# Two GNN layers on one core: rows normalized in one ScalarE pass, and seven of layer 1's blocks in seven products

## The chip, the cores and the metric

The kernel runs on one core of a Trainium2 chip. The engines of a core work side by side, each through its own list of instructions in order: TensorE (PE) multiplies matrices, VectorE (DVE) and ScalarE (ACT) work elementwise, GpSimd (POOL) does small elementwise work and issues gathers, SyncE (SP) issues transfers. They wait for each other by semaphores. The metric is the device time of one execution in microseconds (us), and lower is better. "Time" below is that; a "span" is the time from the first to the last instruction of a profiled execution.

## The reference

Two layers of a graph transformer over N = 2708 nodes with 512 features, 8 heads of 64, and a feed-forward part of width 2048, all in float32. The adjacency matrix has about nine entries in a row. Cut to one layer, which is applied twice with its own weights:

```python
mask = adj + eye(n)
q, k, v = h @ Wq.T + bq, h @ Wk.T + bk, h @ Wv.T + bv        # 8 heads of 64
scores = einsum('nhd,mhd->hnm', q, k) / sqrt(64)
attn = softmax(where(mask == 0, -1e9, scores))
ctx = einsum('hnm,mhd->nhd', attn, v).reshape(n, 512)
h1 = layer_norm(h + ctx @ Wo.T + bo, ln1_g, ln1_b)
ff = relu(h1 @ W1.T + b1) @ W2.T + b2
h2 = layer_norm(h1 + ff, ln2_g, ln2_b)
```

layer_norm subtracts a row's mean, divides by the square root of its variance plus 1e-5, and then multiplies by a gain and adds a shift.

## The kernel before

**Attention by lists.** The kernel makes for each node a list of its neighbours, sorts the nodes by the length of their lists into 22 tiles of 128 rows (the last has 20), and gathers the keys and values of the neighbours from DRAM, a row of 1024 numbers for each node and list place. The longest list of each tile is a constant (CAPS, 3 to 22 places). Attention over a tile runs in chunks of two places: POOL gathers the rows into a buffer kv (L1114), DVE multiplies them by q (L1151) and sums by heads to the scores sc (L1157), ACT takes exponentials p (L1170) and weights the second place's values (L1177), DVE weights the first place's (L1183) and adds both into acc (L1190). ACT's and DVE's last part of a chunk is written behind the scores of the next chunk. At a tile's end DVE adds the two halves and makes the divisor (L1198 to L1213), and ACT writes the context cx (L1221). Gathers are asked about four chunks ahead. The context of a tile lies in one of CXB = 3 places until it is used; attention stops when all are full.

**Blocks.** The 22 tiles are worked off as 11 blocks of two, blocks 0 to 10. A block's feed-forward part is a loop over 16 steps f of 128 hidden numbers each. In a step PE makes pf (the product with W1, four matmuls 128x256, L1578 or L1720), and ACT makes ft = relu(pf + b1) (L1589 or L1731). In a plain block PE adds, three steps behind, ft's product with W2, two matmuls of 128x512 (L1551).

**Seven products.** In blocks 2 to 9 of layer 0 (FORMED = 1 is the last plain one ahead of them), feed_forward_by_seven takes the steps in pairs j = 0 to 6. The pair's product with W2 is a 2x2 product of blocks, which takes eight half-width matmuls of 128x256 when done plainly. It is done in seven (L1710), by Winograd's scheme. For that DVE makes four sums of parts of ft for each pair (L1687 to L1690), written ahead of the chunks of the same step; four sums of W2's quarters are needed for each pair. Three of them (forms) lie in DRAM (form_d) and are loaded by SP for each pair and block (L1672), the fourth (t1) takes W2's quarter b12 in its place. They are made in block 1 (form, L1649 to L1659). At a block's end DVE puts the partial sums together (L1763 to L1768). Steps 14 and 15 stay plain (L1740, L1744).

**Beside the steps.** While block k goes through its steps, the other work is hung into the steps by hand. At f = 10 PE turns the context of the next block's first tile (tp<-cx, L1336) and ACT moves it to cT (L1341); at f = 11 comes its output projection o (L621), then DVE's total h of o and the residual (L1294), the turn of the second tile, and ACT's sum of squares (L1311); at f = 12 the same for the second tile; at f = 13 and 14 the normalization; at f = 15 PE turns the rows (tp<-h) and ACT moves them to hT. The block before has its second normalization (ended) at the steps of TAILS; in layer 0 its rows are then turned (f = 7) and multiplied for layer 1's keys and values (f = 8 and 9, four projections), and written out. In layer 1 they go straight to the output.

**Normalization.** Norm.total has DVE add and sum the row, squares has ACT sum the squares, centred has POOL make the power -1/2 (L1318, L1320) and DVE subtract the mean and multiply by the gain (L1321), scaled has ACT multiply by the power (L1327). Where rows are turned, ACT adds the shift from a column as it moves them. In row form the shift is added by a DMA of POOL's queue that accumulates (L1330). The other form, norm, does all on DVE (L1270 to L1283), for the first and the last block of a layer.

**Order.** The order on each engine is that in which the program writes the instructions. How much attention is written into a step is set by tables: PACE for plain blocks, PACE7 for blocks by seven products, PACES for block 0; 1.0 is one chunk of two places. A context that isn't there when it is needed is finished on the spot (until).

**Border.** In layer 0's last block (10) SP loads layer 1's W1 and W2 as the old ones become free. After it PE projects layer 1's queries until the first contexts are there.

Of the kernel before, what the change touches and what calls it, by code (L numbers as in the profile page):

```python
# [13 lines left out]
ALU = mybir.AluOpType  # L14
# [40 lines left out]
PACE7 = (0.0,) * 4 + (0.6,) + (1.3,) * 4 + (0.6,) * 2 + (0.0,) * 2 + (0.5, 0.8, 2.4)  # L55
TAILS = ((0, 1, 5, 6), (3, 4, 5, 6), (0, 1, 2, 3, 5, 8))
FORMED = 1
# [427 lines left out]
def by_edges(ctx: ExitStack, tc: tile.TileContext, x, xT, adj, layers, out, redo):  # L485
# [71 lines left out]
    form_d = dram.tile([NFC // 2 - 1, 3, P, 2 * P], F32, name="form_d")  # L557
# [582 lines left out]
    class Tile:  # L1140
# [75 lines left out]
        def divided(self):  # L1216
            r = self.r
            cx = at.tile([P, DM], F32, tag="cx", name="cx", bufs=CXB)
# [47 lines left out]
    def norm(z, r, gain, shift=None, st=None):  # L1266
# [9 lines left out]
        nc.gpsimd.tensor_tensor(rd[:r], va[:r], mhalf[:r], ALU.pow)  # L1276
        nc.vector.scalar_tensor_tensor(
            z[:r], z[:r], mv[:r, 0:1], gain[:r], ALU.subtract, ALU.mult
        )
        if shift is None:  # L1280
            nc.vector.tensor_scalar(z[:r], z[:r], rd[:r], None, ALU.mult)
            return
        nc.vector.scalar_tensor_tensor(z[:r], z[:r], rd[:r], shift[:r], ALU.mult, ALU.add)  # L1283

    class Norm:


        def __init__(self, z, r, gain, junk):
            self.z, self.r, self.gain, self.junk = z, r, gain, junk
# [25 lines left out]
        def centred(self):  # L1315
            r, z, nm = self.r, self.z, self.nm
# [4 lines left out]
            nc.vector.scalar_tensor_tensor(  # L1321
                z[:r], z[:r], nm[:r], self.gain[:r], ALU.add, ALU.mult
            )

        def scaled(self):
            r, z = self.r, self.z
            nc.scalar.activation(z[:r], z[:r], AF.Copy, scale=self.rd[:r])  # L1327
# [4 lines left out]
    def flip(z, r, to, shift=None):  # L1332
# [7 lines left out]
        for c in range(NC):  # L1340
            nc.scalar.activation(  # L1341
                to[:, c, :], tp[:, c, :r], AF.Identity, bias=shift[:, c : c + 1]
            )

    class Layer:
# [5 lines left out]
        def load_first(self):  # L1351
# [7 lines left out]
            self.unsettled = raw_columns(w, ("bv", "ln1_b"), place)  # L1359
            self.bv, self.e1 = [col[0] for col in self.unsettled]  # L1360
# [44 lines left out]
        def load_next(self):  # L1405
# [4 lines left out]
            self.unsettled += raw_columns(self.w, ("ln2_b",), place)  # L1410
            self.e2c = self.unsettled[-1][0]
# [64 lines left out]
        def attended(self, block, got, xbs=None, soon=False):  # L1476
# [16 lines left out]
            for i, xb in enumerate(xbs):  # L1493
# [8 lines left out]
                if soon:  # L1502
                    if self.n == 0 and block == blocks[0]:
                        nc.vector.tensor_tensor(h[:r], h[:r], self.bo[:r], ALU.add)
                    norm(h, r, self.g1)
                else:
                    norms.append(Norm(h, r, self.g1, xb).total(parts[-1], last))
# [6 lines left out]
            for one in norms:  # L1514
                one.centred()
# [133 lines left out]
        def form(self, j):  # L1649
# [8 lines left out]
            for i, t in enumerate((t2, t3, t4)):  # L1658
                nc.sync.dma_start(out=form_d[j, i], in_=t)  # L1659
# [523 lines left out]
```

## Time and profile before

| what | value |
|---|---|
| time, median of two runs | 1837.17 us |
| the two runs | 1838.9 and 1835.44 us |
| time of the profiled execution | 1834.85 us |
| its span | 1833.1 us |
| granted clock of TensorE | 0.999 of full speed |

A profile row of the timeline reads: start in us from the span's beginning, duration in us, engine, line of the program, operation, output <- inputs, shapes, and in brackets the idle time just ahead of it with what ended it. PE's matmuls are pipelined and their ends modelled, so the distance between two starts tells what one costs. Rows of one kind that follow each other are merged (x8). A float32 matmul leaves two records, so x8 is four matmuls. A row of the stretches gives for each engine the busy us within the stretch.

### The profile page before, as it was taken

What the parts mean: (1) busy time and instruction counts of PE and PEld (TensorE: products, weight loads), DVE (VectorE), ACT (ScalarE), POOL (GpSimd) and SP (SyncE); (2) the same over time, 40 slices, a digit from 0 to 9 for tenths busy, and PEclk for the clock granted to TensorE, in tenths of its full rate; (3) what the DMA queues carried; (4) which work ended last, traced back from release to release, by engine and by line L of the source; (5) the groups of instructions that cost most, each with busy time, mean ns of one, the idle gap of its engine ahead of it and who ended that gap; (6) DMA issues with size and microseconds to landing.
All of it is one profiled execution on the core that took longest, in us unless ns stands there. A gap on an engine that the chain in (4) does not pass through costs nothing.

```text
span 1833.1 us, 22912 instructions
## 1 busy us (share of the span) xinstructions
PE 1807.7 (99%) x6563; PEld 1161.2 (63%) x6563; DVE 1327.7 (72%) x2271; ACT 1050.6 (57%) x3505; POOL 919.3 (50%) x929
## 2 busy tenths in 40 slices
PE   9999999999999999999999999999999999999998
PEld 4444456566777867767686644666666666666666
DVE  5986768876969778697775147867797787788732
ACT  5770436655656556565664213666676676677641
POOL 3234756645645556365551132454574566567512
PEclk9999999999999999999999999999999999999999
DMA  9997988867878787686863786955675685666511
GB/s 343 376 335 258 370 271 275 240 205 254 263 221 243 239 240 241 201 253 202 248 198 113 230 288 263 321 155 195 213 238 169 228 261 176 220 208 204 154 29 38
DMA packets 172943, 420.73 MB, mean 230 GB/s; under 512 B 19258, under 2 KB 62638, under 8 KB 172808
## 3 DMA queue, kind: packets, MB, share of 16 engines
q0 software_dynamic: 85488, 279.03, 49.1%
q1 hardware_dynamic: 77162, 118.55, 18.7%
q10 hardware_dynamic: 10158, 21.61, 3.1%
q8 instruction: 53, 0.87, 0.2%
q14 instruction: 82, 0.67, 0.1%
HBM read 338.78 MB, written 53.44 MB: 214 GB/s over the span
## 4 chain that ended last, share of the span: by engine, by line
PE 80%; issue 6%; DVE 5%; DMA 3%; ACT 3%; POOL 3%; POOLq 0%; SPq 0%; DVEq 0%; ACTq 0%
PE pf L1578 17%; PE a L1551 17%; PE pf L1720 8%; PE k L621 7%; PE v L621 7%; PE o L621 7%; PE q L621 5%; PE c L1710 4%; PE a L1710 3%; PE tp L1336 2%; DVE kv L1151 1%; ACT kv L1177 1%; DVE sc L1157 1%; POOL kv L1114 1%; DMA kv<-kv_d,listed 1%
## 5 line engine op out<-in xcount | busy, mean ns | idle before, releaser
L1114 POOL DMA_INDIRECT kv<-kv_d,listed x420 | 509.7, 1214 | 282.4 <-issue 108.3
L1578 PE MATMUL pf<-hT,w 128*128 128x256 f32 (+1 forms) x1792 | 393.1, 367 | 0.8 <-ACT ft L1589 0.7
L1578 PEld LDWEIGHTS pf<-hT,w 128*128 128x128 f32 x1792 | 323.5, 190 | 104.4 <-issue 61.0
L1551 PE MATMUL a<-w,ft 128*128 128x512 f32 x800 | 373.5, 592 | 0.1
L1177 ACT ACTIVATE kv<-kv,p 128x64 f32<-128x64 f32 x1232 | 311.0, 335 | 5.0
L1151 DVE TENSOR_TENSOR kv<-kv,q 128x1024 f32<-128x1024 f32 (+1 forms) x222 | 257.4, 1159 | 18.5 <-DMA q<-q_d,ident_i 11.7
L1157 DVE TENSOR_REDUCE sc<-kv 128x16 f32<-128x1024 f32 (+1 forms) x222 | 258.0, 1162 | 7.6
L1190 DVE TENSOR_TENSOR acc<-acc,kv 128x1024 f32<-128x1024 f32 (+2 forms) x178 | 206.3, 1159 | 58.6 <-ACT kv L1177 45.8
L1720 PE MATMUL pf<-hT,w 128*128 128x256 f32 x1024 | 232.9, 379 | 0.0
L1551 PEld LDWEIGHTS a<-w,ft 128*128 128x128 f32 x800 | 150.0, 190 | 113.0 <-issue 102.0
L1720 PEld LDWEIGHTS pf<-hT,w 128*128 128x128 f32 x1024 | 193.9, 190 | 33.3 <-issue 8.1
L1318 POOL TENSOR_SCALAR va<-sq 128x1 f32<-128x1 f32 (+1 forms) x78 | 38.2, 490 | 314.6 <-ACT xb L1311 219.5
L1170 ACT ACTIVATE p<-sc,listed 128x8 f32<-128x8 f32 x420 | 104.0, 296 | 127.8 <-DVE sc L1157 105.6
L1589 ACT ACTIVATE ft<-pf,b 128x256 f32<-128x256 f32 (+1 forms) x208 | 94.6, 458 | 105.3 <-PE pf L1578 96.6
L621 PE MATMUL o<-wo,cT 128*128 128x512 f32 x336 | 150.8, 592 | 0.0
L1183 DVE TENSOR_TENSOR kv<-kv,p 128x512 f32<-128x512 f32 (+1 forms) x178 | 123.2, 692 | 8.0 <-ACT p L1170 7.8
L1294 DVE CUSTOM_DVE_ANT_0 h<-o,xb 128x512 f32<-128x512 f32 x36 | 24.9, 691 | 129.1 <-PE o L621 105.9
L621 PEld LDWEIGHTS o<-wo,cT 128*128 128x128 f32 x336 | 63.6, 190 | 73.2 <-issue 66.5
L1731 ACT ACTIVATE ft<-pf,b 128x256 f32<-128x256 f32 x96 | 44.8, 466 | 100.0 <-PE pf L1720 95.2
L746 DVE MAX8 tops<-code 128x8 f32<-128x247 f32 (+2 forms) x242 | 78.6, 400 | 27.2 <-ACT code L741 27.2
L1330 POOL DMA_DIRECT2D h<-ln_b x86 | 83.6, 1114 | 24.5 <-PE tp L1336 21.8
L1221 ACT ACTIVATE cx<-acc,su 128x64 f32<-128x64 f32 (+1 forms) x352 | 88.3, 333 | 11.8 <-DVE su L1213 8.9
(246 smaller groups left out, 2477.2 us busy)
## 6 DMA issues: line engine op xcount, KB each, us to landing
aj<-in_adj SPq DMA_DIRECT2D x42, 677.0 KB
forms<-form_d SPq DMA_DIRECT2D x168, 128.0 KB
h<-ln_b POOLq DMA_DIRECT2D x83, 256.0 KB
kv_d<-kvs ACTq DMA_DIRECT2D x21, 512.0 KB
xg<-in_xT SPq DMA_DIRECT2D x19, 512.0 KB
w<-in_W SPq DMA_DIRECT2D x16, 512.0 KB
kv<-kv_d,listed POOLq DMA_INDIRECT x420
zT_d<-zT SPq DMA_DIRECT2D x22, 256.0 KB
```

Of the source, the lines that this page charges most:

```text
L621: nc.tensor.matmul(o[:r], xs(c), wm[:, c, :], start=(c == 0), stop=(c == NC - 1))
L1114: return nc.gpsimd.indirect_dma_start(out=to, out_offset=None, in_=table[:, :], in_offset=bass.IndirectOffsetOnAxis(ap=s, axis=0), bounds_ ...
L1151: nc.vector.tensor_tensor(kv[:r, :c, :DM], kv[:r, :c, :DM], self.q[:r].unsqueeze(1).to_broadcast([r, c, DM]), ALU.mult,)
L1157: nc.vector.tensor_reduce(self.sc[:r, s0 : s0 + c, :], kv[:r, :c, :DM].rearrange("p s (h d) -> p s h d", d=DK), AX.X, ALU.add,)
L1170: nc.scalar.activation(p[:r, s, :], self.sc[:r, s, :], AF.Exp, bias=minus[:r, g, s : s + 1])
L1177: nc.scalar.activation(to[:, i, hd], kv[:r, i, DM + h * DK : DM + (h + 1) * DK], AF.Copy, scale=p[:r, s0 + i, h : h + 1],)
L1183: nc.vector.tensor_tensor(to[:, 0, :].rearrange("p (h d) -> p h d", d=DK), kv[:r, 0, DM:].rearrange("p (h d) -> p h d", d=DK), p[:r, s0, : ...
L1190: nc.vector.tensor_tensor(self.acc[:r, :c, :], self.acc[:r, :c, :], kv[:r, :c, DM:], ALU.add)
L1551: nc.tensor.matmul(a[:r, cols], fts[f][:, c0 : c0 + r], self.w2[f // 2][:, f % 2, cols], start=(f == 0), stop=(f == NFC - 1),)
L1578: nc.tensor.matmul(pf[:, :w], self.w1[f // 2][:, c, f % 2 * P : f % 2 * P + P], hT[:, c, :w], start=(c == 0), stop=(c == NC - 1),)
L1710: nc.tensor.matmul(to, left, right, start=start, stop=stop)
L1720: nc.tensor.matmul(pf[:, :W], self.w1[j][:, c, f % 2 * P : f % 2 * P + P], hT[:, c, :], start=(c == 0), stop=(c == NC - 1),)
```

## The change

1. **Normalization in one pass.** Norm.centred becomes power: POOL also multiplies the negative mean by the power, and scaled has ACT do scale and shift by these two in one pass, without DVE. The gain goes to where the shift was: ACT multiplies by a gain column and adds the shift column as it moves turned rows (flip), and in row form POOL multiplies the row by the gain, two tiles one after the other, and then issues the two accumulating DMAs (regained). norm loses an instruction in the form without a shift. Both squares of a block's second normalization stand in one step now, so that its pass on ACT comes a step earlier (TAILS). In layer 0 the stores of keys, values and rows are written in one step.
2. **Layer 1 by seven products.** FORMED is 2 for layer 1, so its blocks 3 to 9 take seven products. The sums of its W2 are made in layer 0's last block, and two of the seven sets behind it (form_apart), into three of the five kv buffers (staged), and stored by SP with t1 as a fourth. In block 2 SP loads t1 into W2's quarter (form_in). PACE7 has a row for layer 1.
3. **Five contexts.** In layer 1 contexts may also lie in the places of the rows bo and bk, and attention runs ahead in the stretch of query projections without the earlier condition.

```diff
-PACE7 = (0.0,) * 4 + (0.6,) + (1.3,) * 4 + (0.6,) * 2 + (0.0,) * 2 + (0.5, 0.8, 2.4)
-TAILS = ((0, 1, 5, 6), (3, 4, 5, 6), (0, 1, 2, 3, 5, 8))
-FORMED = 1
+    (0.0, 0.3, 0.4, 0.5, 0.6, 1.2, 0.7, 1.2, 0.7, 1.2, 0.5, 0.0, 0.0, 1.0, 0.6, 1.8),
+TAILS = ((0, 1, 2), (3, 4, 5), (1, 2, 3, 5, 8), (3, 4, 5, 6, 9))
+FORMED = (1, 2)
+MORE_CX = ("bo", "bk")
...
-        def centred(self):
-            r, z, nm = self.r, self.z, self.nm
+        def power(self):
+            r = self.r
             va = small.tile([P, 1], F32, tag="va", name="va")
             nc.gpsimd.tensor_scalar(va[:r], self.sq[:r], 1.0 / DM, EPS, ALU.mult, ALU.add)
             self.rd = small.tile([P, 1], F32, tag="rd", name="rd")
             nc.gpsimd.tensor_tensor(self.rd[:r], va[:r], mhalf[:r], ALU.pow)
-            nc.vector.scalar_tensor_tensor(
-                z[:r], z[:r], nm[:r], self.gain[:r], ALU.add, ALU.mult
-            )
+            nc.gpsimd.tensor_tensor(self.nm[:r], self.nm[:r], self.rd[:r], ALU.mult)
...
-            nc.scalar.activation(z[:r], z[:r], AF.Copy, scale=self.rd[:r])
+            nc.scalar.activation(
+                z[:r], z[:r], AF.Identity, bias=self.nm[:r], scale=self.rd[:r]
+            )
+    def regained(tiles, gain, row):
+        for z, r in tiles:
+            nc.gpsimd.tensor_tensor(z[:r], z[:r], gain[:r], ALU.mult)
+        for z, r in tiles:
+            nc.gpsimd.dma_start(out=z[:r], in_=row[:r], accum_op=ALU.add)
...
+        def form_apart(self, j, slots):
+            w, W = self.w2[j], 2 * P
+            b11, b12, b21, b22 = w[:, 0, :W], w[:, 0, W:], w[:, 1, :W], w[:, 1, W:]
+            i = 4 * j % len(slots)
+            t2, t3, t4, t1 = slots[i : i + 4]
+            nc.vector.tensor_tensor(t3, b22, b12, ALU.subtract)
+            nc.vector.tensor_tensor(t1, b12, b11, ALU.subtract)
+            nc.vector.tensor_tensor(t2, b22, t1, ALU.subtract)
+            nc.vector.tensor_tensor(t4, b21, t2, ALU.subtract)
+            for i, t in enumerate((t2, t3, t4, t1)):
+                nc.sync.dma_start(out=form_d[self.n][j, i], in_=t)
+        def form_in(self, j):
+            W = 2 * P
+            nc.sync.dma_start(out=self.w2[j][:, 0, W:], in_=form_d[self.n][j, 3])
...
-                if len(got) < 2 or i < 3:
-                    advance(0.65)
+                advance(0.65)
...
-            seven = n == 0 and FORMED < k < NB - 1
+            seven = FORMED[n] < k < NB - 1
...
+                if n > 0 and k == FORMED[n] and f > 4 and f % 2:
+                    now.form_in((f - 5) // 2)
...
+                    if f > 6 and f % 2:
+                        nxt.form_apart((f - 7) // 2, staged)
...
             for _ in range(2):
                 nxt.query(*pool.pop(0))
+                nxt.form_apart(6 - len(pool) % 2, staged)
```

What the change does to the order is shown at three places. First ACT in a block by seven products of layer 0, from the squares of the block before (u, sq) to the turn of its rows for layer 1 (zT); "ft" and "forms" with pf are the relus of steps 4 to 7. Before:

```order
L1311 ACTIVATE u_4993,sq<-h,nm 128x512
L1170 ACTIVATE p<-sc,listed 128x8 x2
L1177 ACTIVATE kv<-kv,p 128x64 x8
L1221 ACTIVATE cx<-acc,su 128x64 x8
L1731 ACTIVATE forms<-pf,b_1157 128x256
L1170 ACTIVATE p<-sc,listed 128x8 x2
L1177 ACTIVATE kv<-kv,p 128x64 x8
L1731 ACTIVATE ft<-pf,b_1157 128x256
L1327 ACTIVATE h<-h,rd 128x512 x2
```

And now:

```order
L1322 ACTIVATE u_5018,sq<-h,nm 128x512 x2
L1776 ACTIVATE forms<-pf,b_1160 128x256
L1176 ACTIVATE p<-sc,listed 128x8 x2
L1183 ACTIVATE kv<-kv,p 128x64 x8
L1230 ACTIVATE cx<-acc,su 128x64 x8
L1776 ACTIVATE forms<-pf,b_1160 128x256
L1336 ACTIVATE h<-h,nm,rd 128x512 x2
L1176 ACTIVATE p<-sc,listed 128x8 x2
L1183 ACTIVATE kv<-kv,p 128x64 x8
```

The pass that scales the rows (h<-h) stands ahead of one chunk's weights and of one relu that it stood behind.

Second, layer 1's block 4 (tiles 6 and 11), which was plain and goes by seven products now: DVE from the fifth sums to the second total h of o. Before, in such a block:

```order
L1157 TENSOR_REDUCE sc<-kv 128x16
L1183 TENSOR_TENSOR kv<-kv,p 128x512
L1190 TENSOR_TENSOR acc<-acc,kv 128x1024
L1294 ISA h,zsum<-o,xb 128x512
L1294 ISA zsum 128x1
L1305 TENSOR_SCALAR nm<-zsum 128x1
L1294 ISA h,zsum<-o,xb 128x512
```

And now, from the last chunk ahead of it:

```order
L1163 TENSOR_REDUCE sc<-kv 128x16
L1189 TENSOR_TENSOR kv<-kv,p 128x512
L1196 TENSOR_TENSOR acc<-acc,kv 128x1024
L1732 TENSOR_TENSOR forms<-ft 128x128
L1733 TENSOR_TENSOR ft<-ft 128x128
L1734 TENSOR_TENSOR forms<-forms,ft 128x128
L1735 TENSOR_TENSOR forms<-ft,forms 128x128
L1305 ISA h,zsum<-o,xb 128x512
L1305 ISA zsum 128x1
L1316 TENSOR_SCALAR nm<-zsum 128x1
```

Sums stand between the chunks and the totals. In the whole block, from one combination to the next, there are seven chunks and five sums ahead of the first total, and four chunks and two sums behind it; in a plain block there are no sums. On ACT at the same place, from the last two chunks to cT (weights of a chunk stand behind the scores of the next):

```order
L1176 ACTIVATE p<-sc,listed 128x8 x2
L1183 ACTIVATE kv<-kv,p 128x64 x8
L1176 ACTIVATE p<-sc,listed 128x8 x2
L1183 ACTIVATE acc<-kv,p 128x64 x8
L1776 ACTIVATE forms<-pf,b_8266 128x256
L1360 ACTIVATE cT<-tp,bv 128x128 x4
```

cT and the relu of its step stand behind the weights of the last chunk but one that DVE has scored, as in the plain block, but after fewer steps of PE.

Third, DVE behind layer 0's last block, where the first two queries of layer 1 (qs) and the last keys (kvs) are moved out of PSUM. Before:

```order
L1453 SCALAR_TENSOR_TENSOR qs<-q,bq 128x512 x2
L1814 TENSOR_TENSOR kvs<-k,bk 20x512
L631 TENSOR_TENSOR kvs<-k,kvs 20x512 x3
L631 TENSOR_TENSOR kvs<-v,kvs 20x512 x3
L1814 TENSOR_TENSOR kvs<-k,bk 128x512
```

And now:

```order
L1472 SCALAR_TENSOR_TENSOR qs<-q,bq 128x512
L1683 TENSOR_TENSOR forms<-w_8450 128x256
L1684 TENSOR_TENSOR forms<-w_8450 128x256
L1685 TENSOR_TENSOR forms<-w_8450,forms 128x256
L1686 TENSOR_TENSOR forms<-w_8450,forms 128x256
L1472 SCALAR_TENSOR_TENSOR qs<-q,bq 128x512
L1683 TENSOR_TENSOR forms<-w_8478 128x256
L1684 TENSOR_TENSOR forms<-w_8478 128x256
L1685 TENSOR_TENSOR forms<-w_8478,forms 128x256
L1686 TENSOR_TENSOR forms<-w_8478,forms 128x256
L1858 TENSOR_TENSOR kvs<-k,bk 20x512
```

Two sets of weight sums stand between the queries and ahead of the keys.

109 lines of the change are left out of this document (64 added, 45 removed).

## The prediction

> **What bounds the kernel now.** First the page: how busy is TensorE, and what does the chain that ended last consist of.
>
> ```profile
> span 1833.1 us, 22912 instructions
> PE 1807.7 (99%) x6563; PEld 1161.2 (63%) x6563; DVE 1327.7 (72%) x2271; ACT 1050.6 (57%) x3505; POOL 919.3 (50%) x929
> PE 80%; issue 6%; DVE 5%; DMA 3%; ACT 3%; POOL 3%; POOLq 0%; SPq 0%; DVEq 0%; ACTq 0%
> ```
>
> PE is busy almost all of the span, so the two things that can shorten the kernel are fewer matmuls and fewer gaps between them. A busy share is an average, so next comes the busy time by stretches: one in layer 0's blocks by seven products, one at the border between the layers, one in layer 1.
>
> ```profile
> core 0: us, PE busy (x) PEld busy (x) DVE busy (x) ACT busy (x) POOL busy (x), PEclk, DMA share, GB/s
> 500.00:600.00 100.00, 98.82 (x393) 71.48 (x392) 79.52 (x133) 60.47 (x217) 54.85 (x53) 1.00 0.81 243
> 1000.00:1100.00 100.00, 99.22 (x393) 54.95 (x392) 28.29 (x52) 19.97 (x60) 26.24 (x28) 1.00 0.76 246
> 1400.00:1500.00 100.00, 100.00 (x357) 65.45 (x356) 80.22 (x107) 71.95 (x262) 65.49 (x59) 1.00 0.71 228
> ```
>
> Layer 1 has no PE gap at all, at a DVE that is already 80% busy; DVE is idle only at the border. Third the timeline of PE: its gaps, its blocks and the price of one product.
>
> ```profile
> 411.96 1.27 PE L1336 MATMUL tp<-ident,h 128*128 128x128 f32 x8 [1.83 <-ACT h L1327]
> 489.42 1.27 PE L1336 MATMUL tp<-ident,h 128*128 128x128 f32 x8 [1.18 <-ACT h L1327]
> 566.45 1.27 PE L1336 MATMUL tp<-ident,h 128*128 128x128 f32 x8 [1.18 <-ACT h L1327]
> 877.11 1.27 PE L1336 MATMUL tp<-ident,h 128*128 128x128 f32 x8 [1.17 <-ACT h L1327]
> ...
> 481.60 0.59 PE L1710 MATMUL a<-forms,ft 128*128 128x256 f32 x2
> 484.63 3.62 PE L1720 MATMUL pf<-hT,w 128*128 128x256 f32 x16
> ...
> 1282.25 7.07 PE L1578 MATMUL pf<-hT,w 128*128 128x256 f32 x32
> 1318.86 3.60 PE L621 MATMUL o<-wo,cT 128*128 128x512 f32 x8
> 1322.29 0.60 PE L1336 MATMUL tp<-ident,cx 128*128 128x128 f32 x4
> 1322.72 1.89 PE L1578 MATMUL pf<-hT,w 128*128 128x256 f32 x8
> 1324.45 1.88 PE L1551 MATMUL a<-w,ft 128*128 128x512 f32 x4
> 1345.96 7.07 PE L1578 MATMUL pf<-hT,w 128*128 128x256 f32 x32
> ```
>
> Starts are what counts here, since ends are modelled. The first four rows are the first three and the last of seven gaps, one for each of layer 0's blocks 2 to 8, in which PE waits for ACT's scaled rows: 1.83 + 3 x 1.18 + 3 x 1.17 = 8.9 us. Seven products take 484.63 - 481.60 = 3.03 us, 0.43 each. A block of layer 1 takes 1345.96 - 1282.25 = 63.7 us; in it a step's pf takes 1.73, an o 3.43, a tp 0.43.
>
> **Part 1: seven products in layer 1.** Eight half-width products (four of 128x512, each two of 0.43) become seven, so each of 7 pairs saves 0.43, a block 3.0 us: PE alone would need 60.7, and seven blocks would give 21.1. That is a gain only if DVE and ACT keep up. Their prices, from layer 0, where the same code runs, and from ACT in layer 1:
>
> ```profile
> 548.44 0.68 DVE L1198 TENSOR_TENSOR acc<-acc 128x512 f32<-128x512 f32 x1
> 549.65 0.37 DVE L1763 TENSOR_TENSOR h<-u,h 128x256 f32<-128x256 f32 x1
> 552.53 0.68 DVE L1294 CUSTOM_DVE_ANT_0 h<-a,h 128x512 f32<-128x512 f32 x1
> 554.12 0.28 DVE L1687 TENSOR_TENSOR forms<-ft 128x128 f32<-128x128 f32 x1
> 563.22 1.22 DVE L1151 TENSOR_TENSOR kv<-kv,q 128x1024 f32<-128x1024 f32 x1
> 565.61 0.68 DVE L1183 TENSOR_TENSOR kv<-kv,p 128x512 f32<-128x512 f32 x1
> 567.53 0.29 DVE L1687 TENSOR_TENSOR forms<-forms 128x128 f32<-128x128 f32 x1
> 568.73 0.69 DVE L1151 TENSOR_TENSOR kv<-kv,q 128x512 f32<-128x512 f32 x1
> 1380.34 0.50 ACT L1170 ACTIVATE p<-sc,listed 128x8 f32<-128x8 f32 x2
> 1380.88 2.02 ACT L1177 ACTIVATE kv<-kv,p 128x64 f32<-128x64 f32 x8
> 1382.80 0.46 ACT L1589 ACTIVATE ft<-pf,b 128x256 f32<-128x256 f32 x1
> 1386.64 1.14 ACT L1341 ACTIVATE cT<-tp,bv 128x128 f32<-128x128 f32 x4 [3.38 <-PE tp L1336]
> ```
>
> By starts: the combination of the products with both totals is 554.12 - 549.65 = 4.5 us; a chunk of attention (two key rows: kv, sc, kvp, acc) is 567.53 - 563.22 = 4.3, of which 1.9 is behind its sc; the four sums of a pair are 568.73 - 567.53 = 1.2; the end of an attention tile is 549.65 - 548.44 = 1.2; the two totals are 554.12 - 552.53 = 1.6 of the 4.5. On ACT a chunk is 1382.80 - 1380.34 = 2.5, a ft some 0.4, a cT 1.1.
>
> A block of layer 1 now asks DVE for 7 x 1.2 = 8.4 us of sums and 2.9 for the combination (4.5 less 1.6 for the totals, which were there before), and gives back four L1321. In the new order the six blocks 3 to 8 hold 10.5, 11, 10, 11.5, 10 and 11 chunks, 10.7 on average; block 9 holds none. So DVE has 10.7 x 4.3 + 8.4 + 4.5 + 1.6 (totals after o) + some 2.4 (tile ends), less 2.6 for the first chunks without acc, about 60 us of work against PE's 60.7. That would just fit if nothing waited. But DVE works in order and has to wait once per block, for o. I follow block 4 by the second piece of order shown above, from the start of the combination: 4.5, then six full chunks, one first chunk of 3.0, a tile end of 1.2 and five sums before the first h, 36; the sc on which ACT's last work before cT hangs comes 7.4 earlier (chunk 4.3, sums 1.2, the end 1.9 of the chunk before): 33.1. ACT: 2.5 + 0.4 + 1.1, to 37.1. PE: o 3.43, tp 0.43, seven products 3.03, pf 1.73, o 3.43, to 49.2. DVE: a total 0.8, four chunks and a sums row, with the tile's end 18.3, to 68.3, where the next combination starts. Block 4 has 11 chunks; at 10.7 a turn is 67.0 us, against 63.7 before. Six such turns cost 6 x 3.3 = +19.8; block 9, without attention, runs at PE's pace, -3.0. So the removed product is not what sets the end: PE waits at o for cT, because ACT's cT stands behind attention that DVE has only just scored. In the plain block PE reaches o 1318.86 - 1282.25 = 36.6 us after its start, about when cT can be there; now it would be there after 12 x 1.73 + 3 x 3.03 + 0.43 = 30.3.
>
> **Part 2: rows normalized in one pass.** DVE loses L1321 (0.75 us by the row below); in layer 0 it was waiting for PE anyway, so that is worth nothing there. ACT's scaled pass moves ahead of one chunk (first piece of order), 2.5 us earlier against gaps of 1.2: I take all 8.9 us as gone. Bounds: 0, if ACT is late for another reason, and 8.9. POOL gets per block four 128x512 products and four small ones.
>
> ```profile
> L959 POOL TENSOR_TENSOR kvs<-kvs,bk 128x512 f32<-128x512 f32 x20 | 25.4, 1271 | 52.8 <-ACT kvs L957 48.1 <-issue 4.7
> 1388.57 0.19 POOL L1318 TENSOR_SCALAR va<-sq 128x1 f32<-128x1 f32 x1 [7.42 <-ACT xb L1311]
> 1395.34 0.75 POOL L1318 TENSOR_SCALAR va<-sq 128x1 f32<-128x1 f32 x1 [5.93 <-ACT xb L1311]
> 1395.29 0.75 DVE L1321 SCALAR_TENSOR_TENSOR h<-h,nm,ln_g 128x512 f32<-128x512 f32 x1 [0.22 <-ACT xb L1311]
> ```
>
> Four at 1.27 and four at about 0.6 make 7.5 us a block; POOL, 65.5 of 100 us busy, goes to some 49 of 67, and its gathers run four chunks (17 us) ahead: nothing on the path by itself. Behind them on POOL stand the additions of the shift row, which are needed ten steps later. But the same va takes 0.19 alone and 0.75 beside a two-operand DVE instruction: the engines hold each other up. A DVE chunk that meets a new product could lose between 0 and 1.27 us; a gain is excluded, since the products are added. All four fall ahead of cT, so the ends are 0 and 5.1 us a block, 0 and 30 over six. In the rows it is POOL that waits, so I stay near the lower end: 1.0 a block, 6.
>
> The Trainium skill, "SBUF — State Buffer", section "Who interferes with whom", says that a DVE instruction with two SBUF inputs contends with a GpSimd instruction that reads SBUF, and that the second to issue blocks fully. By that rule the term is the upper end, and the sum would be 1875 us; the stretched va agrees on POOL's side, and no row here shows DVE as the one that waits.
>
> **Part 3: weight sums in layer 0's last block.** 28 additions of 128x256, about 0.4 us each (L1763), lie where DVE is 28% busy. Only the last two sets (3.4 us) stand between evictions of q (third piece of order), and behind them the eviction of k and, through the PSUM places, PE's next transpose:
>
> ```profile
> 1070.71 0.66 PE L1336 MATMUL tp<-ident,h 128*128 128x128 f32 x4
> 1070.82 0.68 DVE L1814 TENSOR_TENSOR kvs<-k,bk 20x512 f32<-20x512 f32 x1 [0.47 <-PE k L616]
> ```
>
> Bounds 0 and 3.4; I take 2.0, since PE started that transpose without slack. The 28 stores, 7 loads of t1 and 147 loads of forms of 128 KB go through SP: 19 MB over some 420 us is 45 GB/s more on 228, below the 243 of layer 0's blocks, whose forms never held PE by more than 0.2 us; so 0. On SP the forms also stand behind the loads of q, whose places DVE gave up a whole tile earlier: 0. Five contexts instead of three change only how far attention runs ahead: 0 by themselves.
>
> **The sum**, against the profiled execution's own 1834.85 us (2.3 below the median of the two runs, 1837.17): 1834.85 - 8.9 + 19.8 - 3.0 + 6.0 + 2.0 = 1850.8, so 1851.
>
> **Rivals.**
> DVE keeps up (ends on the other side): PE alone sets layer 1, 1834.85 - 8.9 - 21.1 + 2.0 = 1806.9, perhaps up to 1828 where waits are short. It decides if the way from the combination to cT is 6.3 us shorter than my 37.1 (67.0 - 60.7), one and a half chunks. For it: layer 0's blocks run the same products with 80% DVE and no wait for sums. Against: those blocks have 13.7 us more PE work (four projections of 3.43) between the chunks and o.
>
> POOL's products hold DVE fully: 1844.8 + 30 = 1875 (1862 to 1885).
>
> The earlier pass of ACT doesn't end layer 0's gaps, because the power on POOL is now three instructions: 1850.8 + 8.9 = 1860, inside my own range.
>
> **Chances.** My forecast (turns of 65 to 69 us, 1835 to 1862) 0.55; DVE keeps up 0.22; POOL holds DVE 0.15; layer 0's gaps stay 0.08. The range from 1803 to 1870 leaves out a fifth or less: the upper half of the third case and the edge of the second; the likeliest case alone spans 1835 to 1862. Two per cent is 37 us, about what a measurement of this kernel can tell from no change: 1800 and 1874 are the limits. Slower by more takes most of POOL's case, 0.10; faster by more needs DVE to keep up and something else besides, 0.04; within 2% 0.86.
>
> **What would show it.** Right: blocks 3 to 8 of layer 1 start 65 to 69 us apart, with PE idle at o, waiting for ACT's cT, and at pf for ACT's ft, and DVE waiting for PE's second o while over 85% busy; block 9 takes 61; layer 0's gaps before the tp of h are gone and its blocks take 75.8 instead of 77.0. Wrong: layer 1's blocks 61 us apart without PE gaps (first rival), or DVE products stretched from 1.22 to over 2 us beside POOL's (second).

## The result and the profile after

The changed kernel takes 1923.48 us (median of 1922.02 and 1924.94) against 1837.17: a ratio of 1.047, with a 95% interval of 1.0415 to 1.0524. The prediction of 1851 was right in direction and far off in size, outside its range. The profiled execution took 1922.02 us.

First the page of the kernel after: span, busy times, and the chain that ended last.

```profile
span 1920.3 us, 24511 instructions
PE 1827.1 (95%) x6888; PEld 1230.9 (64%) x6888; DVE 1418.3 (74%) x2454; ACT 1085.1 (57%) x3512; POOL 1018.4 (53%) x1093
PE 61%; DVE 17%; ACT 8%; issue 6%; DMA 5%; POOL 2%; SPq 0%; DVEq 0%; POOLq 0%; ACTq 0%
```

PE's share of the chain fell from 80% to 61%; DVE's rose from 5% to 17%, ACT's from 3% to 8%. The stretches of the kernel after tell where (columns as before: busy us of each engine, granted clock, DMA share, GB/s):

```profile
500.00:600.00 100.00, 98.44 (x392) 71.22 (x391) 83.00 (x129) 61.91 (x215) 61.79 (x63) 1.00 0.81 247
800.00:900.00 100.00, 92.12 (x364) 66.87 (x363) 80.51 (x123) 66.02 (x232) 61.54 (x60) 0.97 0.73 220
1400.00:1500.00 100.00, 86.35 (x335) 64.24 (x335) 77.71 (x126) 55.84 (x197) 52.33 (x52) 0.91 0.66 217
1700.00:1800.00 100.00, 88.64 (x349) 66.52 (x349) 85.93 (x137) 60.91 (x216) 54.95 (x54) 0.93 0.66 211
```

In layer 1 PE has gaps, where it had none, and its granted clock is 0.91 to 0.93 instead of 1.00. Four points of the two timelines (the combination of layer 0's block 9 on DVE, and PE's first pf of layer 1's blocks 3, 9 and 10) split the 87 us:

| stretch | before | after | difference | predicted |
|---|---|---|---|---|
| to layer 0's last combination | 1011.0 | 1029.5 | +18.5 | -8.9 |
| from there to block 3 of layer 1 | 335.0 | 341.4 | +6.5 | +2.0 |
| blocks 3 to 8 (per block) | 382.3 (63.7) | 446.7 (74.4) | +64.4 | +19.8 + 6.0 |
| block 9 | 61.6 | 59.0 | -2.6 | -3.0 |
| block 10 to the end | 43.3 | 43.7 | +0.4 | 0 |

Three things are in the traces. First, the waits of layer 0. PE's timeline after, at three of the seven blocks:

```profile
410.00 1.04 PE L1354 MATMUL tp<-ident,h 128*128 128x128 f32 x8
416.99 3.27 PE L627 MATMUL k<-wk,zT 128*128 128x512 f32 x7 [1.20 <-ACT zT L1360]
495.16 3.70 PE L627 MATMUL k<-wk,zT 128*128 128x512 f32 x8 [1.56 <-ACT zT L1360]
813.66 5.40 PE L627 MATMUL k<-wk,zT 128*128 128x512 f32 x8 [4.97 <-ACT zT L1360]
```

No tp of h waits any more, as predicted; but one step later PE's keys wait for zT, the moved rows, as long or longer. ACT shows why. The first row is from before, the four others are from after, at the first of these places: the chunk weights (p, kv) stand ahead of zT as before, and zT itself, which now has two columns (gain and shift), takes 2.88 us where it took 2.14.

```profile
415.22 2.14 ACT L1341 ACTIVATE zT<-tp,ln_b 128x128 f32<-128x128 f32 x8
```

```profile
412.66 0.48 ACT L1176 ACTIVATE p<-sc,listed 128x8 f32<-128x8 f32 x2
413.17 2.02 ACT L1183 ACTIVATE kv<-kv,p 128x64 f32<-128x64 f32 x8
415.10 0.45 ACT L1776 ACTIVATE ft<-pf,b 128x256 f32<-128x256 f32 x1
415.45 2.88 ACT L1360 ACTIVATE zT<-tp,ln_b,ln_g 128x128 f32<-128x128 f32 x8
```

Second, DVE beside POOL's gain products. In the timeline of the kernel after, a pair of products (POOL, L1343) that meets a DVE instruction with two operands in SBUF holds it, and the instruction does not end before the pair does:

```profile
470.59 2.50 POOL L1343 TENSOR_TENSOR h<-h,ln_g 128x512 f32<-128x512 f32 x2
470.69 2.95 DVE L1189 TENSOR_TENSOR acc<-kv,p 128x512 f32<-128x512 f32 x1
1461.91 4.10 DVE L1157 TENSOR_TENSOR kv<-kv,q 128x1024 f32<-128x1024 f32 x1
1462.42 2.50 POOL L1343 TENSOR_TENSOR h<-h,ln_g 128x512 f32<-128x512 f32 x2
1538.05 3.77 DVE L1196 TENSOR_TENSOR acc<-acc,kv 128x1024 f32<-128x1024 f32 x1
1538.24 2.50 POOL L1343 TENSOR_TENSOR h<-h,ln_g 128x512 f32<-128x512 f32 x2
```

The acc<-kv,p of 0.68 us takes 2.95, the kv and acc of 1.22 take 4.10 and 3.77: longer by 2.3 to 2.9 us, about the pair's 2.5. From 380 us on (layer 0's block 2) 30 DVE instructions take over 0.8 us more than the median of their line and shape, 66 us in all; each stands beside products, and 29 end only after them. DVE's groups in layer 1's blocks 3 to 9 (count | busy, mean ns | idle before) show which operations are held; the first row is acc in the kernel before, the others are from after:

```profile
L1190 DVE TENSOR_TENSOR acc<-acc,kv 128x1024 f32<-128x1024 f32 x52 | 64.1, 1233 | 14.7 <-ACT kv L1177 10.3
```

```profile
L1163 DVE TENSOR_REDUCE sc<-kv 128x16 f32<-128x1024 f32 x60 | 73.2, 1220 | 2.0
L1196 DVE TENSOR_TENSOR acc<-acc,kv 128x1024 f32<-128x1024 f32 x51 | 71.1, 1395 | 21.8 <-ACT kv L1183 18.0 <-ACT ft L1776 0.5
L1305 DVE CUSTOM_DVE_ANT_0 h<-o,xb 128x512 f32<-128x512 f32 x13 | 9.0, 691 | 35.8 <-PE o L627 35.8
```

acc, with two operands in SBUF, is up from 1233 to 1395 ns on average; the reduction sc, with one, stays at 1220, and the total of o, one operand of which lies in PSUM, at 691. The Trainium skill, "SBUF — State Buffer", section "Who interferes with whom", has both halves of this: a DVE instruction with two SBUF inputs and a GpSimd instruction that reads SBUF exclude each other, one with at most one SBUF input does not. The trace agrees with it. That the second to issue is the one that blocks, as the prediction has it, does not come out of these rows: 12 of the 30 started 0.2 to 0.5 us ahead of the products, as those at 1461.91 and 1538.05, and were held all the same; once, at 1612.51, it was POOL's product that took 2.24 us. Gathers that come late behind the products are not the loss: from 380 us on DVE's products with q wait for gathered rows for 2.5 us in all, and for 3.9 us before the change.

Third, PE's clock. PE's timeline after, at the o of blocks 3 and 4, and the stretches around the first:

```profile
1402.85 1.99 PE L1765 MATMUL pf<-hT,w 128*128 128x256 f32 x8 [0.50 <-ACT ft L1776]
1409.61 6.13 PE L627 MATMUL o<-wo,cT 128*128 128x512 f32 x8 [4.76 <-ACT cT L1360]
1470.25 3.78 PE L1765 MATMUL pf<-hT,w 128*128 128x256 f32 x8 [3.18 <-ACT ft L1776]
1485.76 5.40 PE L627 MATMUL o<-wo,cT 128*128 128x512 f32 x8 [3.71 <-ACT cT L1360]
```

```profile
1390.00:1400.00 10.00, 8.02 (x37) 6.75 (x36) 9.66 (x17) 7.76 (x31) 7.87 (x8) 1.00 1.03 335
1400.00:1410.00 10.00, 4.74 (x22) 3.66 (x22) 9.48 (x14) 6.64 (x27) 7.91 (x6) 0.89 1.02 381
1410.00:1420.00 10.00, 10.00 (x31) 6.08 (x31) 7.00 (x16) 2.54 (x9) 0.95 (x3) 0.77 0.40 141
```

The forecast wait stands there: PE waits at o for cT and at pf for ft, with DVE 95% busy. But behind the wait o takes 6.13 us instead of 3.60, and the granted clock is 0.89 and 0.77. Ahead of the last 6 us of the span, the trace's clock records have eleven stretches at half clock, of 3.4, 6.8 and once 13.7 us: 10.2 us in layer 0 and 54.6 in layer 1. Before there is none but at the very end.

### The profile page after: what moved, and what is told of

It is laid out like the page before. It is cut to its first block, busy times and chain, and to the rows that moved or that the text cites. A ratio compares the mean times of both kernels' runs of the same rounds, so it can differ in the third digit from the quotient of the medians.

```text
span 1920.3 us, 24511 instructions
## 1 busy us (share of the span) xinstructions
PE 1827.1 (95%) x6888; PEld 1230.9 (64%) x6888; DVE 1418.3 (74%) x2454; ACT 1085.1 (57%) x3512; POOL 1018.4 (53%) x1093
## 4 chain that ended last, share of the span: by engine, by line
PE 61%; DVE 17%; ACT 8%; issue 6%; DMA 5%; POOL 2%; SPq 0%; DVEq 0%; POOLq 0%; ACTq 0%
PE pf L1765 8%; PE o L627 8%; PE pf L1597 8%; PE a L1570 8%; PE v L627 7%; PE k L627 7%; PE q L627 6%; PE c L1755 4%; DVE kv L1157 4%; DVE sc L1163 3%; PE a L1755 3%; ACT kv L1183 3%; DMA kv<-kv_d,listed 2%; DVE acc L1196 2%; PE tp L1354 2%
## 5 line engine op out<-in xcount | busy, mean ns | idle before, releaser
L1765 PE MATMUL pf<-hT,w 128*128 128x256 f32 x1920 | 446.7, 385 | 22.9 <-ACT ft L1776 18.6
L1765 PEld LDWEIGHTS pf<-hT,w 128*128 128x128 f32 x1920 | 366.9, 193 | 90.8 <-ACT ft L1776 23.7
L1196 DVE TENSOR_TENSOR acc<-acc,kv 128x1024 f32<-128x1024 f32 (+2 forms) x178 | 224.3, 1260 | 68.5 <-ACT kv L1183 56.5
L1329 POOL TENSOR_SCALAR va<-sq 128x1 f32<-128x1 f32 (+1 forms) x78 | 20.3, 260 | 330.7 <-ACT xb L1322 221.0
L1597 PE MATMUL pf<-hT,w 128*128 128x256 f32 (+1 forms) x896 | 184.7, 354 | 0.5 <-ACT hT L1360 0.5
L627 PE MATMUL o<-wo,cT 128*128 128x512 f32 x336 | 163.8, 634 | 21.4 <-ACT cT L1360 21.4
L1776 ACT ACTIVATE ft<-pf,b 128x256 f32<-128x256 f32 x180 | 83.5, 466 | 164.6 <-PE pf L1765 158.5
L1570 PE MATMUL a<-w,ft 128*128 128x512 f32 x352 | 165.2, 593 | 0.0
L1343 POOL TENSOR_TENSOR h<-h,ln_g 128x512 f32<-128x512 f32 (+1 forms) x86 | 109.4, 1294 | 31.9 <-PE tp L1354 19.1
L627 PE MATMUL k<-wk,zT 128*128 128x512 f32 x168 | 81.9, 633 | 20.8 <-ACT zT L1360 13.4
L1570 PEld LDWEIGHTS a<-w,ft 128*128 128x128 f32 x352 | 65.5, 190 | 47.8 <-issue 43.4
```

What stands on the lines that cost most here:

```text
L627: nc.tensor.matmul(o[:r], xs(c), wm[:, c, :], start=(c == 0), stop=(c == NC - 1))
L1196: nc.vector.tensor_tensor(self.acc[:r, :c, :], self.acc[:r, :c, :], kv[:r, :c, DM:], ALU.add)
L1343: nc.gpsimd.tensor_tensor(z[:r], z[:r], gain[:r], ALU.mult)
L1570: nc.tensor.matmul(a[:r, cols], fts[f][:, c0 : c0 + r], self.w2[f // 2][:, f % 2, cols], start=(f == 0), stop=(f == NFC - 1),)
L1597: nc.tensor.matmul(pf[:, :w], self.w1[f // 2][:, c, f % 2 * P : f % 2 * P + P], hT[:, c, :w], start=(c == 0), stop=(c == NC - 1),)
L1765: nc.tensor.matmul(pf[:, :W], self.w1[j][:, c, f % 2 * P : f % 2 * P + P], hT[:, c, :], start=(c == 0), stop=(c == NC - 1),)
```

## The experiments

All times are medians; the kernel before, run beside them on the same chips, had 1838.5, 1836.3, 1837.8 and 1836.2 us. Its single executions lie between 1834 and 1841 us, so 2 or 3 us between two single traces are weak evidence.

**The gain without POOL's products.** In regained:

```diff
-        for z, r in tiles:
-            nc.gpsimd.tensor_tensor(z[:r], z[:r], gain[:r], ALU.mult)
```

> Leaves out the multiplication of the row form by the gain (all ones in this data): POOL's four products 128x512 per block are gone, all else is the changed kernel. If POOL's products hold DVE (DVE's two-input instructions stretched to 3.8 us in the changed kernel, some 34 us in layer 0 and 23 in layer 1 above their usual 1.22, 0.68 and 0.28), then no stretched instruction is left, layer 0's blocks go from 80 us back to 77 or less, layer 1's turns from 74 to about 68, and the time is 1860 to 1885 us. If the order alone is what costs (waits moved in layer 0, DVE's work in layer 1), the time stays above 1910.

1882.98 us, ratio 1.0238 (1.0214 to 1.0261): 40.5 less. Layer 0's last combination falls from 1029.5 to 1013.2, blocks 3 to 8 from 74.4 to 70.5 each, 24.0 together. The products cost 40 us, 16 of them in layer 0. But layer 1's blocks did not come down to 68, and layer 0 still ends 2 us later than before the change: from 380 us on PE's idle time in it is 10.5 us instead of 13.4, but 10.2 us go at half clock behind the waits that are left, where before had none.

**Layer 1 plain, all else as changed.**

```diff
-FORMED = (1, 2)
+FORMED = (1, 10)
```

(and without form_apart, form_in and prepared in layer 1).

> Layer 1's blocks are plain again and the weight sums for layer 1 are not made; the one-pass normalization with POOL's products and the five contexts stay. If the seven products in layer 1 cost what the traces show between block 3 and the end (some 62 us), the time is 1855 to 1868 us: before's 1837, plus layer 0's loss of 18 to 20, plus a little for POOL's products in layer 1, where PE has no gap to lose. If POOL's products hold DVE enough to make plain blocks late as well, layer 1's blocks go above 65 us and the time is over 1870. If five contexts and the order of the border matter, its start of layer 1 is still 6 us late.

1863.77 us, 1.0137 (1.0117 to 1.0156). PE's timeline in layer 1 of this kernel:

```profile
1565.45 7.07 PE L1597 MATMUL pf<-hT,w 128*128 128x256 f32 x32
1629.16 7.07 PE L1597 MATMUL pf<-hT,w 128*128 128x256 f32 x32
```

63.7 us a block, as before, with POOL's products beside them: the plain block hides them wholly. Of the 29.9 us between the spans, 28.4 lie ahead of block 3: 23.7 in layer 0, and 4.6 on the way from there to block 3, although no weight sums are made.

**Useless matmuls in PE's gaps.** In the loop of steps, in layer 1's blocks 3 to 8:

```diff
+                if seven and n > 0 and more and k < NB - 2 and f in (8, 10):
+                    now.filled(hT_now, 3 if f == 8 else 4)
```

> In layer 1's blocks 3 to 8 PE makes three useless products 128x512 after step 8 and four after step 10 (2.6 and 3.4 us at full clock), into a place that nobody reads, just where it waits for ACT's ft and cT. If the halved clock behind PE's gaps (54 us of half clock in layer 1, worth up to 27) lies on the path, the half clock goes from layer 1's blocks and the time falls by 10 to 25, to 1898 to 1913 us. If DVE's work alone sets the turn, the clock recovers and the time stays within 5 of 1923. If the fillers themselves come in the way, it rises by up to 6 x 6 = 36.

1919.29 us (1.0431, 1.0403 to 1.046), 4 less, which the two intervals do not tell from nothing. Half clock in layer 1's blocks 3 to 8 falls from 54.6 to 20.5 us, PE's idle time in them from 50.1 to 26.8 us, and a block takes 73.9 instead of 74.4. The half clock that is gone is worth some 17 us of PE's time and the idle time 23; the 42 fillers, 36 us at 0.86 each, take nearly all of it. So giving PE its clock back did not shorten the turn; what the half clock costs by itself is not settled, since the fillers also stand in PE's way.

**The former normalization with seven products in layer 1** (centred and scaled as before the change; the order and the rest as changed).

> The changed kernel with the former normalization: DVE subtracts the mean and multiplies by the gain (four more DVE instructions of 0.75 us a block), ACT only scales, POOL has no products; seven products in layer 1, the weight sums, five contexts and the new order stay. If POOL's products are the larger part of the loss, this is well below 1923: 1865 to 1890, some 5 to 15 above the kernel without the gain, since DVE has 3 us more work in a turn. If the one pass is worth what it was made for, it is above 1923.

1883.15 us, 1.0245 (1.0224 to 1.0266), the same as the one pass without the products, where 5 to 15 more were expected. DVE's four instructions of 0.75 us a block are not felt, so the pass that takes them away gains nothing.

**The same, layer 1 plain.**

> The former normalization and layer 1 plain, no weight sums for layer 1; of the change there remain five contexts and the order (TAILS, stores, attention beside the queries). With the three others this makes a square of two by two: seven products (with or without) and POOL's gain products (with or without). If each cost stands by itself, this is 1864 - 40 = 1824; if the two costs add up only where an engine has no slack (layer 1 plain hides POOL's products, as its blocks of 63.7 us show), it is 1837 to 1843: before's time, 1.6 less in layer 0, and 4 to 6 more at the border, where the loads of zT come late.

1838.7 us, 1.0011 (1.0 to 1.0022). Order and five contexts cost 2 us, 0 to 4 by the interval. The square:

| | layer 1 plain | seven products in layer 1 |
|---|---|---|
| former normalization | 1838.7 | 1883.2 |
| one pass, POOL's products | 1863.8 | 1923.5 |

The seven products cost 44.5 us, POOL's products 25.1, both together 84.8: 15 more than the sum, since plain blocks hide POOL's products and the others don't.

**The same work, otherwise paced.** On the kernel with the former normalization:

```diff
-    (0.0, 0.3, 0.4, 0.5, 0.6, 1.2, 0.7, 1.2, 0.7, 1.2, 0.5, 0.0, 0.0, 1.0, 0.6, 1.8),
+    (0.2, 0.1, 0.2, 0.3, 0.5, 0.5, 0.6, 0.4, 0.3, 1.0, 1.2, 0.7, 0.7, 0.6, 1.1, 1.7),
```

The place that this edit aims at, in block 6 of the kernel without POOL's products (timeline, all engines): the combination, ACT's cT, PE's o, DVE's totals, and the next combination.

```profile
1572.08 0.43 DVE L1806 TENSOR_TENSOR h<-u,h 128x256 f32<-128x256 f32 x1 [1.41 <-ACT u L1805]
1611.82 1.11 ACT L1358 ACTIVATE cT<-tp,bv 128x128 f32<-128x128 f32 x4
1612.22 6.71 PE L627 MATMUL o<-wo,cT 128*128 128x512 f32 x8 [3.70 <-ACT cT L1358]
1618.96 0.69 DVE L1305 CUSTOM_DVE_ANT_0 h<-o,xb 128x512 f32<-128x512 f32 x1 [3.34 <-PE o L627]
1622.06 0.29 DVE L1730 TENSOR_TENSOR forms<-forms 128x128 f32<-128x128 f32 x1 [2.14 <-PE c L1753]
1627.58 0.69 DVE L1305 CUSTOM_DVE_ANT_0 h<-o,xb 128x512 f32<-128x512 f32 x1 [4.30 <-PE o L627]
1649.24 0.37 DVE L1806 TENSOR_TENSOR h<-u,h 128x256 f32<-128x256 f32 x1
```

From the combination to cT 39.7 us of chunks and sums; then DVE has nothing to do for 3.34 + 2.14 + 4.30 = 9.8 us while PE makes o.

> The kernel with the former normalization (1883 us) and another row of PACE7 for layer 1: of some ten chunks per block 4.1 instead of 6.8 are written ahead of f = 10, 2.6 instead of 0.5 at f = 10 to 12, where DVE waited some 10 us per turn for PE's o. The work is the same. If the way from the combination over the chunks to cT and o sets the turn, turns fall from 70 to 61 to 64 us, PE's gaps and the half clock in layer 1 go, and the time is 1832 to 1850. If DVE's amount of work sets it (60 to 63 us a turn without waits) together with ACT, it stays within 10 of 1883.

1861.27 us, 1.0112 (1.008 to 1.0145): 22 less with the same work in all. Blocks 3 to 8 take 66.9 us instead of 71.4, and PE's 18.5 us of waits at o for cT in them are gone. So the way over the chunks to o did hold the turn. But not all of the gain is the order's: the row also writes less into these blocks. They score 60 chunks instead of 64, and the other four, some 17 us of DVE at 4.3 each, fall to block 9, which takes 64.2 us instead of 59.0. The run does not tell the two apart. The expected 1832 to 1850 was not reached; another wait grew in the place of the old one (PE's timeline of this kernel):

```profile
1512.96 0.70 PE L1753 MATMUL a<-forms 128*128 128x256 f32 x2 [1.39 <-DMA forms<-form_d]
1514.75 1.18 PE L1753 MATMUL c<-forms 128*128 128x256 f32 x2 [1.09 <-DMA forms<-form_d]
1581.58 0.67 PE L1753 MATMUL c<-forms 128*128 128x256 f32 x2 [1.01 <-DMA forms<-form_d]
```

The loaded forms come late, 12 us of waits over six blocks where it was 3, with half clock behind some of them.

**Only block 9 by seven** (FORMED = (1, 8), former normalization).

> The kernel with the former normalization, layer 1 plain but for block 9, beside which no attention runs, so only that block goes by seven products. If the removed products pay wherever DVE is free, block 9 takes 60.7 us instead of 63.7 and the time is 3 us below that of the kernel with all of layer 1 plain run beside it: about 1838 against 1841. If the change of form costs its own (loads of forms, the combination), the two are equal.

1843.03 us, 1.0032 (1.002 to 1.0044), 4 more than all plain beside it, where 3 less were expected. The way from layer 0's last combination to block 3 takes 342.5 us instead of 336.7, since all the weight sums are made for this one block, and the block itself takes 63.0, not 60.7, nor the 61.6 that it takes plain: PE waits 2.08 us in it for ft, and 3.4 us go at half clock.

**Another pace in layer 0 too.** On the kernel of the other pace:

```diff
-    (0.0,) * 4 + (0.6,) + (1.3,) * 4 + (0.6,) * 2 + (0.0,) * 2 + (0.5, 0.8, 2.4),
+    (0.0,) * 4 + (0.6, 1.0, 0.6, 1.3, 1.3, 1.2, 1.0) + (0.0,) * 2 + (0.5, 0.8, 2.4),
```

> As the kernel with the other pace in layer 1, and in layer 0's row chunks moved from f = 5 and 6 to f = 9 and 10 (1.3, 1.3 become 1.0, 0.6; 0.6, 0.6 become 1.2, 1.0). If layer 0's waits of PE at k are chunk weights ahead of zT on ACT, those waits (0.7 to 3.6 us a block) go and the time is 4 to 8 us below that kernel's. If zT waits for something else, or the chunks moved come in the way of cT, it is the same or some us more.

1848.34 us, 1.0056 (1.0038 to 1.0073), 13 less, where 4 to 8 were expected; its runs scatter from 1838.7 to 1858, and the profiled one is the slowest. In it layer 0's last combination moves from 1012.5 to 998.2, and PE's waits at k are gone. Then the same row alone in the kernel before, and in the kernel with the former normalization and layer 1 plain:

> The kernel before with one edit: in layer 0's row of the pace chunks move from f = 5 and 6 to f = 9 and 10. If what PE waits for in layer 0's blocks (8.9 us at tp, 4.4 at k) is ACT, held by chunk weights that are written ahead of the scaled rows and of zT, these waits go and layer 0 ends 10 to 13 us earlier: 1824 to 1829 us. If the pace helped only together with the new order of TAILS, it stays within 4 of the kernel before.

> The same row of the pace in the kernel with the former normalization and layer 1 plain (five contexts and the new order stay). If the gain is that of layer 0 alone, 1838.7 less 8 to 12, 1826 to 1831 us, and the two kernels of this pair tell whether the order of TAILS adds anything: they should be within 3 us of each other.

1830.14 us, 0.9962 (0.9947 to 0.9977), and 1826.5, 0.9942 (0.9927 to 0.9957): the second is the fastest of all, the first missed its 1824 to 1829 by 1 us. Beside the second, seven products in layer 1 cost 22 us even with both paces (1848.3). The page of the second, and a row of PE's timeline of the first:

```profile
PE 1805.8 (99%) x6566; PEld 1162.2 (64%) x6566; DVE 1327.3 (73%) x2274; ACT 1049.3 (58%) x3505; POOL 922.8 (51%) x929
PE 92%; DVE 2%; issue 2%; DMA 1%; POOL 1%; ACT 1%; POOLq 0%; SPq 0%; DVEq 0%; ACTq 0%
```

```profile
566.99 1.27 PE L1336 MATMUL tp<-ident,h 128*128 128x128 f32 x8 [1.17 <-ACT h L1327]
```

In the kernel before the pace takes away the waits at k only, those at tp stay, and layer 0's last combination is only 2 us earlier (1008.8), not 10 to 13; with the earlier pass (TAILS) both go (999.4). Each edit alone leaves the other wait. Only 3.6 us lie between the two medians. In the traces the second loses on the way to block 3, which takes 338.0 us and 334.7 in the first: PE waits there 3.14 us for a transfer of zT.

**POOL's two products apart.** Each followed by its own transfer's issue:

```diff
         for z, r in tiles:
             nc.gpsimd.tensor_tensor(z[:r], z[:r], gain[:r], ALU.mult)
-        for z, r in tiles:
             nc.gpsimd.dma_start(out=z[:r], in_=row[:r], accum_op=ALU.add)
```

> The changed kernel with POOL's two gain products of a pair apart: each is followed at once by the issue of its own accumulating transfer (about 1 us). In the changed kernel one DVE instruction is held for the whole 2.5 us of both. If the hold lasts as long as products follow each other, DVE gets in between now, no held instruction is longer than 1.22 + 1.27 = 2.5 us, and the time falls if the second product meets DVE in an instruction that it does not hold (the reduce sc, PSUM work), by up to half of the 40 us, or stays if DVE is held twice. If the hold has nothing to do with the products' time, the held instructions stay at 3.8 us.

1931.31 us, 1.0516 (1.0487 to 1.0545), 8 more, within what the two intervals allow for none. In its timeline two DVE instructions of 0.68 us are held, by 0.9 and 2.0 us:

```profile
393.09 1.28 POOL L1343 TENSOR_TENSOR h<-h,ln_g 128x512 f32<-128x512 f32 x1
393.37 1.56 DVE L1189 TENSOR_TENSOR acc<-kv,p 128x512 f32<-128x512 f32 x1
394.85 2.68 DVE L1204 TENSOR_TENSOR acc<-acc 128x512 f32<-128x512 f32 x1
395.35 1.62 POOL L1343 TENSOR_TENSOR h<-h,ln_g 128x512 f32<-128x512 f32 x1
```

Nothing is longer than 2.8 us now (2.5 was expected at most), but 53 instructions take over 0.8 us more than usual instead of 30, 78 us in all instead of 66. The hold goes with the products, and apart they catch DVE twice.

**The pass alone** (former best, with ACT's one pass, the gain of the row form left out).

> The one-pass normalization by itself: as the kernel with the former normalization, layer 1 plain and the other pace in layer 0 (1826.5 us), but with ACT's one pass; the multiplication of the row form by the gain (all ones in this data) is left out, so POOL has no products. If the pass is worth something where POOL doesn't pay for it (DVE 3 us a block less), it is 4 to 15 us below 1826.5. If PE sets layer 0 by then, as the gaps that are gone say, it is the same within 4; the turned rows take ACT 2.9 instead of 2.1 us for eight.

1828.2 us, 0.9959 (0.9945 to 0.9972): no better than the 1826.5 with the former normalization. Where PE sets the pace, DVE's 3 us a block are worth nothing.

## Why the prediction was wrong, step by step

**What bounds the kernel** was read rightly: PE, without gaps in layer 1, at a DVE with little to spare.

**Part 1, seven products.** The mechanism is as forecast: chunks and sums on DVE, cT on ACT, o, the totals, the next combination. Its size was taken too low: 67.0 us a turn, where 70.5 are left without POOL's products. The block that the prediction follows, block 4, shows two terms that were too small. These are PE's first o and DVE's waits behind the totals in the kernel without POOL's products, where the combination starts at 1429.8, the second total at 1480.78 and the next combination at 1504.53:

```profile
1465.39 6.74 PE L627 MATMUL o<-wo,cT 128*128 128x512 f32 x8 [3.71 <-ACT cT L1358]
1491.60 1.22 DVE L1196 TENSOR_TENSOR acc<-acc,kv 128x1024 f32<-128x1024 f32 x1 [1.48 <-ACT kv L1183]
1496.82 0.69 DVE L1189 TENSOR_TENSOR kv<-kv,p 128x512 f32<-128x512 f32 x1 [1.61 <-ACT p L1176]
1499.07 1.22 DVE L1196 TENSOR_TENSOR acc<-acc,kv 128x1024 f32<-128x1024 f32 x1 [1.55 <-ACT kv L1183]
```

cT ends 36.3 us after the combination, near the 37.1 forecast. But the o behind the wait takes 6.74 us, mostly at half clock, and not 3.43; and from the second total to the next combination 23.7 us pass and not 19.1, since DVE waits 4.6 us for ACT's p and kv. The forecast priced these chunks at DVE's 4.3 us alone. So the turn is 74.7 us and not 68.3. Waits of PE for loaded forms, 11.8 us in blocks 3 to 8 of that kernel, had no term either. Block 9 came as forecast, -2.6 for -3.0.

**Part 2, one pass, failed twice.** "I take all 8.9 us as gone": the gaps at tp are gone, but the text did not follow ACT to its next work. zT stands behind the same chunk weights, and the wait moved to k; without POOL's products layer 0 still ends 2 us later than before. It took the pace of layer 0 to gain it. And "in the rows it is POOL that waits, so I stay near the lower end: 1.0 a block, 6": it is DVE that is held, nearly always for the whole pair of products. The upper end (5.1 a block) was nearer; what was measured is 24.0 us in blocks 3 to 8, four a block. A further error is in the count: the ends were worked out for six blocks of layer 1, but POOL multiplies in layer 0's blocks too, where the text gave DVE's time no worth. There the products cost another 16: from 380 us on PE is idle for 24.6 us in layer 0 with them and 10.5 without, and of the difference 5.0 lie at k for zT, and 5.0 where PE waits for DVE to move kvs.

**Part 3, weight sums.** 2.0 forecast for the way to block 3, 6.5 measured. How much of it is the sums' is not settled: beside POOL's products the way takes 341.4 us with them and 339.6 without, with the former normalization 342.0 and 336.7, and 335.0 before. Two zeros failed. The first is the 0 for SP. In SP's timeline after, the stores of the sums (L1688) stand ahead of the loads of zTs, from which PE makes the first queries:

```profile
1065.71 2.40 SPq L1688 DMA_DIRECT2D form_d<-forms  x4
1070.81 2.31 SPq L1688 DMA_DIRECT2D form_d<-forms  x4
1075.44 4.35 SPq L1442 DMA_DIRECT2D zTs<-zT_d  x7
```

and PE waits for these loads: 1.56 us at 1081.50. Every kernel with the sums has this wait, none without them does. The loads of forms were no 0 either, and their working does not hold: 45 GB/s on top of 228 is 273, not below 243. PE waits 3.7 us for them in blocks 3 to 8 of the changed kernel, and 12 where other waits are fewer (without POOL's products, or at the other pace). The second is the 0 for the rest of the change: PE waits 2.63 us for a transfer of zT at 1149, and 1.7 to 3.2 us in the kernels with the new order and five contexts but no sums; before it waited there for no transfer.

**The clock** had no term. In the trace before, the granted clock is 1.00 up to the last 7 us, so no row spoke of it; but the forecast itself put gaps of several us into PE's work. The Trainium skill, "TensorE: Matmul & The Clock Gate", section "HAM oscillation — how this bites in real kernels", warns of PE gaps above some 3.4 us, behind which the clock is halved. The trace agrees in kind: half clock comes in pieces of 3.4 to 13.7 us, here behind gaps of 2 to 6 us. It does not show that limit: half clock follows a gap of 1.98 us at 1535.2, and none follows one of 3.59 us at 798.9 in the kernel with the former normalization and layer 1 plain.

**The sum**: layer 0 was off by 27 us, blocks 3 to 8 by 39, the border by 4.5. With the trace without POOL's products the 71 us that the sum lacked split into the turns (20.6), the products in blocks 3 to 8 (18.0) and in layer 0 (16.3), the gaps of layer 0 (11.1), the border (4.5) and less than 1 for the rest. The second rival, POOL's products holding DVE, was priced at 30 us for six blocks, was true at 40 for the whole kernel (24 in the six), and came on top of the forecast's own case, not in its place: the chances were given to cases that exclude each other where the mechanisms added up, and more than added up (the 15 us of the square).

## What to carry to other kernels

An elementwise product that is moved to GpSimd is not free for VectorE: count each of its instructions, in every stage, as time taken from VectorE's two-operand work, and ask in which stages that time has cover. A wait that is taken away from one step is worth something only if the step behind it doesn't hang on the same queue; here the earlier pass alone gained nothing, the other pace alone 8 us, and both together 11. Fewer matmuls gain nothing where the engine that feeds them is already 80% busy and works in order: move its work to where it waits, before giving it more.

## What the hardware showed that was not expected

- POOL's products of 128x512 with both operands in SBUF hold a DVE instruction with two SBUF operands nearly always until they end, also one that started up to 0.5 us ahead of them, and two products in a row hold one DVE instruction for both (0.68 us become 2.95); apart, they hold two. One-operand reductions (1220 ns) and sums from PSUM (691 ns) are not touched.
- Gaps of 2 to 6 us in PE can be followed by 3.4 to 13.7 us at half clock, in which an o of four 128x512 takes up to 6.7 us instead of 3.6. Not all are: gaps of 2.63 us (at 1146.7, after) and of 3.59 (the kernel with layer 1 plain and the former normalization) were followed by none. Filling the gaps with useless matmuls took 34 us of half clock away and won no more than 4.
- ACT moves eight 128x128 pieces with a shift column in 2.14 us, with gain and shift columns in 2.88.
